# Conditioned attention on one core: the last step by halves of its queries, denominators by folds on VectorE and GpSimd

## The chip, the core and the metric

The kernel runs on one core of a Trainium2 chip. The core has engines that each work through their own queue in order: TensorE (PE in the profile; its weight loads are PEld), VectorE (DVE), ScalarE (ACT), GpSimd (POOL), and SyncE (SP), which here issues DMAs. They wait for each other through semaphores. Operands lie in SBUF, products of PE land in PSUM, which has eight banks of 512 float32 columns on 128 partitions. The metric is the device time in microseconds of one execution, as the median of several; lower is better.

## The reference

For 8 batches of 512 rows and 512 columns, 16 heads of 32 columns, `x + attention(x, cond)` is computed in float32. Cut to what matters:

```python
Q = split_heads(x @ Wq.T + bq); K = split_heads(x @ Wk.T + bk); V = split_heads(x @ Wv.T + bv)
cQ = Q + split_heads(cond @ Wq.T + bq)
cK = K + split_heads(cond @ Wk.T + bk)
attn = softmax(cQ @ cK.T / sqrt(32))          # over the keys
out = x + merge_heads(attn @ V)
```

## The kernel before

**Steps.** The work goes in 32 steps: step `t` is batch `t // 4` and a group of four heads `t % 4`, that is 128 columns of the output. In a step the scores of each head are 512 by 512. The four heads use 32 rows, or 32 columns, of PE each, so that four matmuls stand side by side. Scores are made with the keys on the partitions, so that the exponentials can go straight into the product with V, and the row maxima, found in a pass ahead, are taken off by a small bfloat16 product with ones (`onesb`). Most steps get their denominators from the exponentials of that first pass. The last two steps, 30 and 31 (`T - 2` and `T - 1`), don't: their exponentials are summed by explicit additions and a product with a matrix of ones.

**The order** is written out by hand: each engine gets its instructions in the order of the code, with `bank(i)` naming PSUM banks one by one. Code that stands later on an engine waits for all that stands ahead of it there.

**A block of keys.** `exponentials(t, kc, at)` (L748) makes the scores of 128 keys (`kc` of 0 to 3) against all 512 queries: four products with `onesb` (L753) and four of K with Q (L756), one for each head, into four banks, then four exponentials of 128x512 on ACT (L766), two heads to a chunk of 1024 columns. `times_v` (L821) multiplies such a chunk with V, four matmuls of 512 columns, adding up in one bank over the four blocks; its result has the head's 32 columns on the partitions and the queries along the free side. `times_ones` (L848) does the same with ones, which gives the denominators in the same layout.

**Sums.** `sum_of(t, to, kc, on, prs)` (L1274) adds the exponentials of block `kc` to a running sum, 128x1024 for each pair of heads, on the engine `on`. Step 30 sums in `acc`, step 31 in `acc2`. Before, one such sum of step 30 is on POOL (L1386) and all others are on DVE. For step 31 blocks 0 to 2 are added up and the fourth goes to the ones by itself (L1436).

**The end of step 30 and 31.** Step 30 is turned by DVE in 32x32 blocks (L1416, L1421), divided (L1423), its residual is added on POOL (L1424), and four DMAs store it (`store_30`, L1426). Such DMAs go by `spread`: 32 partitions, runs of 32 columns, 64 KB each. Step 31 is treated as a whole: the denominators are copied by ACT (L1442), the residual `xr` times the denominators is made by DVE (L1443), both parts of `out` times denominators are added (L1452), PE turns them back in 128x128 blocks (L920, L1454), DVE takes reciprocals (L1457) and multiplies (L1462), and two DMAs of 128 KB store them (L1468). The residual of step 31 is not loaded: it is the transposed `x` that the projections used (L195).

**What stands ahead.** The row maxima of step 31 are found during step 30 (`crossed`, L1288). `send_sums` (L1070) turns, divides and stores steps 28 and 29: DVE turns (L912), POOL multiplies and adds (L913, L914), SP issues four stores of 64 KB (L917). `late_part(i)` (L1048) names eight spare pieces of 128x512 in the store of the exponentials, and `xc` is a buffer that the last projections have left.

Of the kernel before, what the change touches and what calls it, by code (L numbers as in the profile page):

```python
# [17 lines left out]
def kernel(  # L18
# [39 lines left out]
    P = 128  # L58
# [57 lines left out]
    def banks(i, n=1):  # L116

        row = row_of[0] or [at_end[j] for j in TURNS[turn[0]]]
        j = row[i]
        if n == 1:  # L120
            return psum[:, j, :]
        k = row[i + 1]
        return psum[:, j : k + 1 : k - j, :]
# [585 lines left out]
    def split_max(t, on=nc.gpsimd):  # L709

        if t >= T:
            return
        m, sp = nmax[t], split[t % 2]
        rest = op.tile([P, NS, HG, 1], F32, tag="rest", name=f"rest_{t}")
        on.tensor_copy(sp[:, :, :, 0:1], m)
        on.tensor_tensor(rest, m, sp[:, :, :, 0:1], ALU.subtract)
        on.tensor_copy(sp[:, :, :, 1:2], rest)
        on.tensor_tensor(sp[:, :, :, 2:3], rest, sp[:, :, :, 1:2], ALU.subtract)
# [338 lines left out]
    def part_of(t, pt, of):  # L1057

        for kc in of:
            times_v(t, kc, pt, of)  # L1060
        parts[t] = stage.tile([P, NC, D], F32, tag="w", name="parts")[:, 0, :]
        nc.scalar.copy(parts[t], pt)
# [7 lines left out]
    def send_sums(t, of, den):  # L1070
        rec = op.tile([P, NB, 1], F32, tag="recs", name=f"recs_{t}")
        nc.vector.reciprocal(rec, den)
        send(t, of, rec)
# [200 lines left out]
    def sum_of(t, to, kc, on, prs=range(NP)):  # L1274
        for pr in prs:
            if kc == 1:
                on.tensor_tensor(to[pr], es[t, 0, pr], es[t, 1, pr], ALU.add)  # L1277
            else:
                on.tensor_tensor(to[pr], to[pr], es[t, kc, pr], ALU.add)  # L1279
# [5 lines left out]
    def row(i):  # L1285
        turn[0] = 8 + i

    def crossed(t, kc, qc, u=None):  # L1288


        u = u or t + 1
        open_max(u)
        bank = [banks(i) for i in range(HG)]

        def maxima(js):
            for j in js:
                row_scores(u, qc, j, banks(HG + j))

        def scores(js):
            for j in js:  # L1300
                r = slice(j * HD, j * HD + 3)
                nc.tensor.matmul(bank[j], onesb[r, :], maxT[t][r, :], start=True, stop=False)
            for j in js:
                r = slice(j * HD, (j + 1) * HD)
                nc.tensor.matmul(
                    bank[j],
                    qkT["k", t][r, kc * P : (kc + 1) * P],
                    qkT["q", t][r, :],
                    start=False,
                    stop=True,  # L1310
                )

        maxima((0, 1))
        scores((2, 3))
        scores((0, 1))
        maxima((2, 3))
        for pr in (1, 0):
            e = es[t, kc, pr] = chunk()
            for i in range(2):
                nc.scalar.activation(e[:, i, :], bank[pr * 2 + i], AF.Exp)  # L1320
        for j in range(2):
            nc.vector.tensor_reduce(
                nmax[u][:, qc, j : j + 1, 0], banks(HG + j), AX.X, ALU.max, negate=True
            )
        row_max_of(u, qc, 1, banks(HG + 2, 2))
# [54 lines left out]
    spread_sums(apart, banks(1))  # L1380
    den = denominators_of(t - 1, banks(1))
    send_sums(t - 1, whole[t - 1], den)
    row(1)
    crossed(t, 1, 2)
    acc = room_for_sums(t)
    sum_of(t, acc, 1, nc.gpsimd, [1])  # L1386
    part_of(t, banks(2), [0])
    row(2)
    crossed(t, 2, 3)
    split_max(t + 1, nc.vector)  # L1390
    pa, rest = banks(2), [1, 2, 3]
    times_v(t, 1, pa, rest)
# [2 lines left out]
    transpose_max(t + 1, bank(5), nc.vector.tensor_copy)  # L1395
    times_v(t, 2, pa, rest)
    sum_of(t, acc, 1, nc.vector, [0])
    sum_of(t, acc, 2, nc.vector)

    t = T - 1  # L1400
    exponentials(t, 0, (2, 3, 0, 1))
    times_v(t - 1, 3, pa, rest)
    nc.vector.tensor_tensor(parts[t - 1], pa, parts[t - 1], ALU.add)
    sum_of(t - 1, acc, 3, nc.vector)
    exponentials(t, 1, (7, 4, 5, 2))
    pv = bank(3)
    times_v(t, 0, pv)
    acc2 = room_for_sums(t)
    sum_of(t, acc2, 1, nc.vector)
    exponentials(t, 2, (0, 1, 7, 6))  # L1410
    times_v(t, 1, pv)
    pd = bank(5)
    times_ones(acc, pd, True, True)
    sum_of(t, acc2, 2, nc.vector)
    den = late_part(3).rearrange("p (f e) -> p f e", e=BL)
    nc.vector.transpose(den.rearrange("p f e -> p (f e)"), pd)  # L1416

    rec = op.tile([P, NB, 1], F32, tag="recs", name=f"recs_{t - 1}")
    nc.vector.reciprocal(rec, den[:, :, 0:1])
    y30 = op.tile([P, NB, BL], F32, tag="res", name=f"res_{t - 1}")  # L1420
    nc.vector.transpose(y30.rearrange("p f e -> p (f e)"), parts[t - 1])  # L1421
    x30 = xr.pop(t - 1)
    nc.vector.tensor_tensor(y30, y30, rec.broadcast_to([P, NB, BL]), ALU.mult)  # L1423
    nc.gpsimd.tensor_tensor(y30, y30, x30, ALU.add)  # L1424
# [1 line left out]
    def store_30(queue, hs):  # L1426
        b, g = divmod(t - 1, G)
        for h in hs:
            queue.dma_start(spread(out[b], g * P + h * BL), y30[h * BL : (h + 1) * BL])

    store_30(nc.sync, (0, 1))
    exponentials(t, 3, (4, 2, 0, 1))
    times_v(t, 2, pv)
    pd = bank(7)
    times_ones(acc2, pd, True, False)
    times_ones([es[t, 3, pr] for pr in range(NP)], pd, False, True)  # L1436
    times_v(t, 3, pv)

    part_x = late_part(6)
    den = late_part(5)  # L1440
    two = [slice(0, HS), slice(HS, S)]
    nc.scalar.copy(den, pd)  # L1442
    nc.vector.tensor_tensor(part_x, pd, xr[t], ALU.mult)  # L1443
    store_30(nc.scalar, (2, 3))
    oT = late_part(4)
    y = late[0][:, 1, :].rearrange("p (c s) -> p c s", c=NS)
    rec = op.tile([P, NS, HG, 1], F32, tag="rec", name="rec")
    pi, po = bank(6), [bank(4), bank(2)]
    b, g = divmod(t, G)
    untranspose(den, pi)  # L1450
    for i in range(2):
        nc.vector.tensor_tensor(oT[:, two[i]], pv[:, two[i]], part_x[:, two[i]], ALU.add)  # L1452
        for qc in (i * 2, i * 2 + 1):
            nc.tensor.transpose(  # L1454
                po[i][:, qc * P : (qc + 1) * P], oT[:, qc * P : (qc + 1) * P], ident
            )
    nc.vector.reciprocal(  # L1457
        rec, pi.rearrange("p (c h e) -> p c h e", c=NS, h=HG)[:, :, :, 0:1]
    )
    for i in range(2):  # L1460
        cs = slice(i * 2, i * 2 + 2)
        nc.vector.tensor_tensor(  # L1462
            y[:, cs].rearrange("p c (h e) -> p c h e", h=HG),
            po[i][:, two[i]].rearrange("p (c h e) -> p c h e", c=2, h=HG),
            rec[:, cs].broadcast_to([P, 2, HG, HD]),
            ALU.mult,
        )
        (nc.scalar, nc.sync)[i].dma_start(  # L1468
            out[b].rearrange("(c p) d -> p c d", p=P)[:, cs, g * P : (g + 1) * P], y[:, cs]
        )  # L1470


# [29 lines left out]
```

## Time and profile before

| | us |
|---|---|
| median of 3 runs | 649.41 (649.35 to 650.63) |
| profiled execution | 649.67 |
| its span | 647.8 |

| engine | busy us | share of the span |
|---|---|---|
| PE | 641.7 | 99% |
| DVE | 600.3 | 93% |
| ACT | 533.5 | 82% |
| POOL | 409.9 | 63% |

The span is what the profiler sees from the first to the last instruction of the program; the execution's own time is 1.87 us more. PE is busy nearly all the time, but matmuls overlap, so that a busy PE is no measure of how closely they follow each other: the starts of the groups tell that. The averages say nothing of the last 25 us, in which the change lies; there one reads the timeline, engine by engine. In the rows of the timeline the columns are the start, the time from the first start to the last end of the group, the engine and line, the operation, the names and shapes, the count, and in brackets how long the engine had been idle and what released it. One float32 matmul shows as two records.

### The profile page before, as it was taken

What the parts mean: (1) busy time and instruction counts of PE and PEld (TensorE: products, weight loads), DVE (VectorE), ACT (ScalarE), POOL (GpSimd) and SP (SyncE); (2) the same over time, 40 slices, a digit from 0 to 9 for tenths busy, and PEclk for the clock granted to TensorE, in tenths of its full rate; (3) what the DMA queues carried; (4) which work ended last, traced back from release to release, by engine and by line L of the source; (5) the groups of instructions that cost most, each with busy time, mean ns of one, the idle gap of its engine ahead of it and who ended that gap; (6) DMA issues with size and microseconds to landing.
All of it is one profiled execution on the core that took longest, in us unless ns stands there. A gap on an engine that the chain in (4) does not pass through costs nothing. (4 is left out here: it accounts for less than half of the span.)

```text
span 647.8 us, 24814 instructions
## 1 busy us (share of the span) xinstructions
PE 641.7 (99%) x9856; PEld 357.3 (55%) x9856; DVE 600.3 (93%) x845; ACT 533.5 (82%) x1364; POOL 409.9 (63%) x651
## 2 busy tenths in 40 slices
PE   9999999999999999999999999999999999999997
PEld 8445555556555555555555555555655555555541
DVE  3799999999999999999999999999999999999887
ACT  2479888889888889888888988898988888898564
POOL 3633655686765775668576776568767577675650
PEclk9999999999999999999999999999999999999999
DMA  7615588888978788877878978878898767796831
GB/s 191 107 26 85 128 164 171 172 171 191 180 158 172 161 180 175 183 165 164 185 171 174 198 150 185 165 173 169 180 195 158 156 144 163 159 189 149 192 63 34
DMA packets 248457, 102.02 MB, mean 157 GB/s; under 512 B 229962, under 2 KB 230474, under 8 KB 248340
## 3 DMA queue, kind: packets, MB, share of 16 engines
q1 hardware_dynamic: 234196, 65.54, 53.6%
q0 software_dynamic: 12384, 33.83, 20.3%
q8 instruction: 78, 1.28, 0.8%
q10 hardware_dynamic: 1760, 1.05, 0.5%
q14 instruction: 39, 0.32, 0.2%
HBM read 19.75 MB, written 8.39 MB: 43 GB/s over the span
## 5 line engine op out<-in xcount | busy, mean ns | idle before, releaser
L593 DVE TENSOR_REDUCE nmax<-psum 128x1 f32<-128x512 f32 x279 | 177.6, 675 | 9.2 <-PE psum L641 4.9
L701 ACT ACTIVATE psum<-psum,nmax 128x512 f32<-128x512 f32 x248 | 165.1, 678 | 3.6 <-DVE nmax L593 3.0
L641 PE MATMUL psum<-kT,qT 32*128 32x512 f32 x1024 | 162.0, 613 | 0.0
L701 ACT ACTIVATE store<-psum,nmax 128x512 f32<-128x512 f32 x204 | 139.5, 700 | 25.0 <-DVE nmax L593 24.8
L682 POOL DMA_DIRECT2D store<-store x258 | 128.6, 503 | 47.2 <-DMA store<-store 28.8
L799 ACT ACTIVATE store<-psum 128x512 f32<-128x512 f32 x232 | 119.8, 603 | 33.4 <-PE psum L785 33.4
L660 DVE STREAM_TRANSPOSE store<-store 128x1024 f32<-128x1024 f32 x116 | 138.9, 1217 | 0.0
L650 DVE TENSOR_REDUCE nmax<-psum 128x2 f32<-128x1024 f32 x98 | 118.9, 1213 | 0.0
L840 PE MATMUL psum<-store,v 128*32 128x256 f32 x1856 | 106.8, 381 | 0.2 <-ACT store L1320 0.2
L840 PEld LDWEIGHTS psum<-store,v 128*32 128x32 f32 x1856 | 57.3, 110 | 57.2 <-ACT wT_q L632 21.2
L913 POOL TENSOR_TENSOR res<-res,recs 128x512 f32<-128x512 f32 x30 | 31.3, 1045 | 90.8 <-DVE res L912 90.8
L785 PE MATMUL psum<-qT,kT 32*128 32x256 f32 x928 | 83.8, 374 | 0.0
L641 PEld LDWEIGHTS psum<-kT,qT 32*128 32x128 f32 x1024 | 61.6, 184 | 35.4 <-issue 17.8
L785 PEld LDWEIGHTS psum<-qT,kT 32*128 32x128 f32 x928 | 60.9, 184 | 5.6 <-issue 0.3
L701 ACT ACTIVATION_READ_ACCUMULATOR psum<-psum,nmax 128x1 f32 x248 | 55.1, 222 | 0.0
L203 POOL TENSOR_TENSOR xr<-xr,bvs 128x512 f32<-128x512 f32 x30 | 38.4, 1282 | 15.6 <-DMA x<-in_x_dram 12.8
L462 PE MATMUL psum<-wc_v,xc 128*32 128x256 f32 x768 | 47.7, 379 | 0.0
L462 PE MATMUL psum<-xc,wc_q 128*32 128x256 f32 x720 | 44.7, 379 | 0.0
L462 PE MATMUL psum<-xc,wc_k 128*32 128x256 f32 x720 | 44.5, 379 | 0.0
L701 ACT ACTIVATION_READ_ACCUMULATOR store<-psum,nmax 128x1 f32 x204 | 44.4, 217 | 0.0
L914 POOL TENSOR_TENSOR res<-res,xr 128x512 f32<-128x512 f32 x30 | 38.3, 1277 | 2.3
L462 PE MATMUL psum<-xT,wT_k 128*32 128x256 f32 x480 | 34.5, 382 | 0.0
(191 smaller groups left out, 972.5 us busy)
## 6 DMA issues: line engine op xcount, KB each, us to landing
store<-store SPq DMA_DIRECT2D x264, 128.0 KB, 2.6
store<-store POOLq DMA_DIRECT2D x258, 128.0 KB, 3.8
out_dram<-res SPq DMA_DIRECT2D x122, 64.0 KB, 3.6
xr<-in_x_dram SPq DMA_DIRECT2D x120, 64.0 KB, 4.4
x<-in_x_dram SPq DMA_DIRECT2D x112, 64.0 KB, 3.3
w_q<-in_L_cond_Wq_dram SPq DMA_DIRECT2D x4, 256.0 KB, 3.9
w_v<-in_L_cond_Wv_dram SPq DMA_DIRECT2D x16, 64.0 KB, 2.5
w_k<-in_L_cond_Wk_dram SPq DMA_DIRECT2D x16, 48.0 KB, 2.6
```

The source lines that it names most:

```text
L203: nc.gpsimd.tensor_tensor(xr[t], xr[t], bias, ALU.add)
L462: nc.tensor.matmul(pt[r], still[:, r], moving, start=(kc == kcs[0]), stop=(kc == kcs[-1]))
L593: nc.vector.tensor_reduce(nmax[t][:, qc, j : j + 1, 0], pt, AX.X, ALU.max, negate=True)
L641: nc.tensor.matmul(pt, qkT["q", t][r, qc * P : (qc + 1) * P], qkT["k", t][r, :], start=True, stop=True,)
L650: nc.vector.tensor_reduce(nmax[t][:, qc, pr * 2 : pr * 2 + 2, 0], pt, AX.X, ALU.max, negate=True)
L660: nc.vector.transpose(e, e)
L682: (nc.gpsimd if here else nc.sync).dma_start(to, of)
L701: nc.scalar.activation(to, of, AF.Exp, bias=nmax[t][:, qc, j, :], accum_out=sums[t][:, qc, j, :],)
L785: nc.tensor.matmul(banks(j)[:, i * HS : (i + 1) * HS], qkT["k", t][r, kc * P : (kc + 1) * P], qkT["q", t][r, KQ * P :], start=False, stop= ...
L799: nc.scalar.activation(e[:, j], banks(j), AF.Exp)
L840: nc.tensor.matmul(pt[j * HD : (j + 1) * HD, half * HS : (half + 1) * HS], vs[b % 2][:, kc, (g * HG + j) * HD : (g * HG + j + 1) * HD], e, ...
L914: nc.gpsimd.tensor_tensor(y, y, xr.pop(t), ALU.add)
```

## The change

Step 31 goes by halves of the queries, `q` = 0 and 1, of 256 columns, and by halves of the keys: each of the four blocks (`last_scores`) makes two key blocks of 128 against one half of the queries, which fills four banks of 512 columns as before. The products with V and with ones are of 256 columns.

For each block the two key blocks in a chunk are folded: `fold` adds the two 256-column parts of each head, 128x512 for a pair of heads. The folds of block (0, 0) go to POOL and those of (0, 1) to DVE, which then adds the two (`of_a`); those of (1, 0) go one to DVE and one to POOL (`of_b`); block (1, 1) isn't folded but goes to the ones in both parts.

The first half of the queries, `y_a`, is turned by DVE straight from PSUM, divided and given its residual by POOL, and stored by four DMAs of 32 KB on SP. Its residual, `x_a`, is loaded by four DMAs on SP behind the stores of step 29, and its bias is added on POOL behind the sum of step 30 that was on POOL before. The second half keeps the way of before, at 256 columns, with one DMA.

For step 30 the second pair's sums of blocks 2 and 3 go from DVE to POOL. Its product with ones, which stood ahead of the last scores, goes behind them and behind the ones of the first half. Its turn (L1421) comes earlier on DVE.

```diff
@@ -1380,13 +1380,24 @@
     spread_sums(apart, banks(1))
     den = denominators_of(t - 1, banks(1))
     send_sums(t - 1, whole[t - 1], den)
+    last_b, last_g = divmod(t + 1, G)
+    for h in range(HG):
+        nc.sync.dma_start(
+            late_part(7)[h * BL : (h + 1) * BL, :HS].rearrange("p (f e) -> p f e", e=BL),
+            spread(x[last_b], last_g * P + h * BL)[:, : NB // 2],
+        )
     row(1)
     crossed(t, 1, 2)
     acc = room_for_sums(t)
     sum_of(t, acc, 1, nc.gpsimd, [1])
+    x_a = late_part(7)[:, :HS].rearrange("p (f e) -> p f e", e=BL)
+    nc.gpsimd.tensor_tensor(
+        x_a, x_a, bvs[:, last_g, :].unsqueeze(1).broadcast_to([P, NB // 2, BL]), ALU.add
+    )
     part_of(t, banks(2), [0])
     row(2)
     crossed(t, 2, 3)
+    sum_of(t, acc, 2, nc.gpsimd, [1])
     split_max(t + 1, nc.vector)
     pa, rest = banks(2), [1, 2, 3]
     times_v(t, 1, pa, rest)
@@ -1395,30 +1406,117 @@
     transpose_max(t + 1, bank(5), nc.vector.tensor_copy)
     times_v(t, 2, pa, rest)
     sum_of(t, acc, 1, nc.vector, [0])
-    sum_of(t, acc, 2, nc.vector)
+    sum_of(t, acc, 2, nc.vector, [0])
+    sum_of(t, acc, 3, nc.vector, [0])
+    sum_of(t, acc, 3, nc.gpsimd, [1])
 
     t = T - 1
-    exponentials(t, 0, (2, 3, 0, 1))
+    b, g = divmod(t, G)
+    ef = {}
+
+    def last_scores(q, half, at):
+
+        bank = [bank_of(i) for i in at]
+        qs = slice(q * HS, (q + 1) * HS)
+        for j in range(HG):
+            r = slice(j * HD, j * HD + 3)
+            nc.tensor.matmul(
+                bank[j],
+                onesb[r, :],
+                maxT[t][r, qs].unsqueeze(1).broadcast_to([3, 2, HS]),
+                start=True,
+                stop=False,
+            )
+        for i in range(2):
+            kc = half * 2 + i
+            for j in range(HG):
+                r = slice(j * HD, (j + 1) * HD)
+                nc.tensor.matmul(
+                    bank[j][:, i * HS : (i + 1) * HS],
+                    qkT["k", t][r, kc * P : (kc + 1) * P],
+                    qkT["q", t][r, qs],
+                    start=False,
+                    stop=(i == 1),
+                )
+        for pr in range(NP):
+            e = ef[q, half, pr] = chunk()
+            for i in range(2):
+                nc.scalar.activation(e[:, i, :], bank[pr * 2 + i], AF.Exp)
+
+    def last_v(q, half, pt):
+        for i in range(2):
+            kc = half * 2 + i
+            for j in range(HG):
+                nc.tensor.matmul(
+                    pt[j * HD : (j + 1) * HD, :HS],
+                    vs[b % 2][:, kc, (g * HG + j) * HD : (g * HG + j + 1) * HD],
+                    ef[q, half, j // 2][:, j % 2, i * HS : (i + 1) * HS],
+                    start=(kc == 0),
+                    stop=(kc == NS - 1),
+                )
+
+    def last_ones(of, pt, start, stop):
+        for j in range(HG):
+            nc.tensor.matmul(
+                pt[j * HD : (j + 1) * HD, :HS],
+                ones[:, :HD],
+                of[j // 2][:, j % 2],
+                start=start,
+                stop=stop,
+            )
+
+    def in_two(q, half, pr):
+        return ef[q, half, pr].rearrange("p h (i s) -> p i h s", i=2)
+
+    def fold(q, half, pr, to, on):
+        e = in_two(q, half, pr)
+        on.tensor_tensor(to, e[:, 0], e[:, 1], ALU.add)
+
+    of_a = [xc[:, pr] for pr in range(NP)]
+    of_a1 = [xc[:, 2 + pr] for pr in range(NP)]
+    of_b = room_for_sums(t)[0].rearrange("p c (r s) -> p (c r) s", r=2)
+    of_b = [of_b[:, pr * 2 : pr * 2 + 2] for pr in range(NP)]
+    NH = NB // 2
+    x_a = late_part(7)[:, :HS].rearrange("p (f e) -> p f e", e=BL)
+    den_a = late_part(7)[:, HS:].rearrange("p (f e) -> p f e", e=BL)
+
+    last_scores(0, 0, (2, 3, 0, 1))
     times_v(t - 1, 3, pa, rest)
     nc.vector.tensor_tensor(parts[t - 1], pa, parts[t - 1], ALU.add)
-    sum_of(t - 1, acc, 3, nc.vector)
-    exponentials(t, 1, (7, 4, 5, 2))
-    pv = bank(3)
-    times_v(t, 0, pv)
-    acc2 = room_for_sums(t)
-    sum_of(t, acc2, 1, nc.vector)
-    exponentials(t, 2, (0, 1, 7, 6))
-    times_v(t, 1, pv)
-    pd = bank(5)
+    y30 = op.tile([P, NB, BL], F32, tag="res", name=f"res_{t - 1}")
+    nc.vector.transpose(y30.rearrange("p f e -> p (f e)"), parts[t - 1])
+    for pr in range(NP):
+        fold(0, 0, pr, of_a[pr], nc.gpsimd)
+    last_scores(0, 1, (7, 4, 5, 2))
+    pva = bank(3)
+    last_v(0, 0, pva)
+    for pr in range(NP):
+        fold(0, 1, pr, of_a1[pr], nc.vector)
+    last_scores(1, 0, (0, 1, 7, 6))
+    last_v(0, 1, pva)
+    for pr in range(NP):
+        nc.vector.tensor_tensor(of_a[pr], of_a[pr], of_a1[pr], ALU.add)
+    y_a = op.tile([P, NB, BL], F32, tag="res", name=f"res_{t}")[:, :NH]
+    nc.vector.transpose(y_a.rearrange("p f e -> p (f e)"), pva[:, :HS])
+    fold(1, 0, 0, of_b[0], nc.vector)
+    fold(1, 0, 1, of_b[1], nc.gpsimd)
+    last_scores(1, 1, (4, 5, 2, 0))
+    pda = bank(3)
+    last_ones(of_a, pda, True, True)
+    pd = bank(1)
     times_ones(acc, pd, True, True)
-    sum_of(t, acc2, 2, nc.vector)
+    nc.vector.transpose(den_a.rearrange("p f e -> p (f e)"), pda[:, :HS])
+    rec_a = op.tile([P, NB, 1], F32, tag="recs", name=f"recs_{t}")[:, :NH]
+    nc.vector.reciprocal(rec_a, den_a[:, :, 0:1])
+    nc.gpsimd.tensor_tensor(y_a, y_a, rec_a.broadcast_to([P, NH, BL]), ALU.mult)
+    nc.gpsimd.tensor_tensor(y_a, y_a, x_a, ALU.add)
+    for h in range(HG):
+        nc.sync.dma_start(spread(out[b], g * P + h * BL)[:, :NH], y_a[h * BL : (h + 1) * BL])
+
     den = late_part(3).rearrange("p (f e) -> p f e", e=BL)
     nc.vector.transpose(den.rearrange("p f e -> p (f e)"), pd)
-
-    rec = op.tile([P, NB, 1], F32, tag="recs", name=f"recs_{t - 1}")
+    rec = op.tile([P, NB, 1], F32, tag="den", name=f"recs_{t - 1}")
     nc.vector.reciprocal(rec, den[:, :, 0:1])
-    y30 = op.tile([P, NB, BL], F32, tag="res", name=f"res_{t - 1}")
-    nc.vector.transpose(y30.rearrange("p f e -> p (f e)"), parts[t - 1])
     x30 = xr.pop(t - 1)
     nc.vector.tensor_tensor(y30, y30, rec.broadcast_to([P, NB, BL]), ALU.mult)
     nc.gpsimd.tensor_tensor(y30, y30, x30, ALU.add)
@@ -1428,46 +1526,40 @@
         for h in hs:
             queue.dma_start(spread(out[b], g * P + h * BL), y30[h * BL : (h + 1) * BL])
 
+    pvb, pdb = bank(6), bank(7)
+    last_v(1, 0, pvb)
+    last_ones(of_b, pdb, True, False)
+    for i in range(2):
+        last_ones([in_two(1, 1, pr)[:, i] for pr in range(NP)], pdb, False, i == 1)
+    last_v(1, 1, pvb)
+
+    part_x = late_part(6)[:, :HS]
+    den = late_part(5)[:, :HS]
+    oT = late_part(4)[:, :HS]
+    nc.vector.tensor_tensor(part_x, pdb[:, :HS], xr[t][:, HS:], ALU.mult)
+    nc.scalar.copy(den, pdb[:, :HS])
     store_30(nc.sync, (0, 1))
-    exponentials(t, 3, (4, 2, 0, 1))
-    times_v(t, 2, pv)
-    pd = bank(7)
-    times_ones(acc2, pd, True, False)
-    times_ones([es[t, 3, pr] for pr in range(NP)], pd, False, True)
-    times_v(t, 3, pv)
-
-    part_x = late_part(6)
-    den = late_part(5)
-    two = [slice(0, HS), slice(HS, S)]
-    nc.scalar.copy(den, pd)
-    nc.vector.tensor_tensor(part_x, pd, xr[t], ALU.mult)
     store_30(nc.scalar, (2, 3))
-    oT = late_part(4)
-    y = late[0][:, 1, :].rearrange("p (c s) -> p c s", c=NS)
-    rec = op.tile([P, NS, HG, 1], F32, tag="rec", name="rec")
-    pi, po = bank(6), [bank(4), bank(2)]
-    b, g = divmod(t, G)
-    untranspose(den, pi)
+    pi, po = bank(4), bank(2)
     for i in range(2):
-        nc.vector.tensor_tensor(oT[:, two[i]], pv[:, two[i]], part_x[:, two[i]], ALU.add)
-        for qc in (i * 2, i * 2 + 1):
-            nc.tensor.transpose(
-                po[i][:, qc * P : (qc + 1) * P], oT[:, qc * P : (qc + 1) * P], ident
-            )
+        nc.tensor.transpose(pi[:, i * P : (i + 1) * P], den[:, i * P : (i + 1) * P], ident)
+    nc.vector.tensor_tensor(oT, pvb[:, :HS], part_x, ALU.add)
+    for i in range(2):
+        nc.tensor.transpose(po[:, i * P : (i + 1) * P], oT[:, i * P : (i + 1) * P], ident)
+    rec = op.tile([P, 2, HG, 1], F32, tag="rec", name="rec")
     nc.vector.reciprocal(
-        rec, pi.rearrange("p (c h e) -> p c h e", c=NS, h=HG)[:, :, :, 0:1]
+        rec, pi[:, :HS].rearrange("p (c h e) -> p c h e", c=2, h=HG)[:, :, :, 0:1]
     )
-    for i in range(2):
-        cs = slice(i * 2, i * 2 + 2)
-        nc.vector.tensor_tensor(
-            y[:, cs].rearrange("p c (h e) -> p c h e", h=HG),
-            po[i][:, two[i]].rearrange("p (c h e) -> p c h e", c=2, h=HG),
-            rec[:, cs].broadcast_to([P, 2, HG, HD]),
-            ALU.mult,
-        )
-        (nc.scalar, nc.sync)[i].dma_start(
-            out[b].rearrange("(c p) d -> p c d", p=P)[:, cs, g * P : (g + 1) * P], y[:, cs]
-        )
+    y = late[0][:, 1, :HS].rearrange("p (c s) -> p c s", c=2)
+    nc.vector.tensor_tensor(
+        y.rearrange("p c (h e) -> p c h e", h=HG),
+        po[:, :HS].rearrange("p (c h e) -> p c h e", c=2, h=HG),
+        rec.broadcast_to([P, 2, HG, HD]),
+        ALU.mult,
+    )
+    nc.sync.dma_start(
+        out[b].rearrange("(c p) d -> p c d", p=P)[:, 2:, g * P : (g + 1) * P], y
+    )
 
 
 # ---- launch: one core; inputs and outputs as the reference has them ----
```

## What was predicted from it

> **What bounds the kernel now.** I read the busy time by stretches first, then the chain that ended last, then the timeline of each engine over the last 25 us.
>
> ```profile
> 630.00:640.00 10.00, 9.92 (x92) 2.50 (x92) 10.00 (x10) 8.26 (x16) 0.00 (x0) 1.00 0.01 2
> 640.00:648.00 8.00, 3.63 (x28) 1.28 (x20) 4.03 (x10) 0.58 (x1) 1.28 (x1) 0.88 0.32 67
> ```
>
> The columns are the length, then busy us and count for PE, PEld, DVE, ACT and POOL, the granted clock, and DMA. In the last full stretch PE and DVE are both full and POOL does nothing; after 640 everything drains.
>
> ```profile
> 638.23 1.24 DVE acc L1279
> ...
> 639.51 1.48 PE psum L850 x10
> ...
> 641.42 0.86 PE psum L824 x6
> ...
> 642.89 0.76 DVE store L1452 x2
> ...
> 643.92 0.42 DVE store L1462
> ```
>
> The chain goes through DVE's last sum for the denominators, ending 639.47, then 2.77 us of PE to 642.28, then the turn, the division and the store.
>
> ```profile
> 632.28 1.08 PE L824 MATMUL psum<-store,v 128*32 128x512 f32 x8
> 633.29 0.40 PE L753 MATMUL psum<-maxT,onesb 3*128 3x512 bf16 x4
> ...
> 634.47 1.07 PE L824 MATMUL psum<-store,v 128*32 128x512 f32 x8
> 635.36 1.04 PE L850 MATMUL psum<-acc,ones 128*32 128x512 f32 x8
> 636.33 0.40 PE L753 MATMUL psum<-maxT,onesb 3*128 3x512 bf16 x4
> ...
> 637.52 1.07 PE L824 MATMUL psum<-store,v 128*32 128x512 f32 x8
> 638.40 1.73 PE L850 MATMUL psum<-acc,ones 128*32 128x512 f32 x6
> ```
>
> Starts matter here, for matmuls overlap: a burst of four 512-column products with V or the ones takes 0.88 us (637.52 to 638.40), 1.0 us ahead of a change to scores (632.28 to 633.29), and a block of scores 1.18 us (633.29 to 634.47). From 638.40 PE has three bursts, 2.6 us, and ends after 3.88: about 1.2 us are lost waiting for DVE. That loss is what the change can remove ahead of the end.
>
> **The change part by part.** *The same PE work in other pieces.* 256-column matmuls are in the trace:
>
> ```profile
> 610.64 1.04 PE L785 MATMUL psum<-qT,kT 32*128 32x256 f32 x16
> ...
> 611.61 1.07 PE L840 MATMUL psum<-store,v 128*32 128x256 f32 x16
> ```
>
> Twice as many records take the same 1.04 and 1.07 us as the 512-column rows, so halving costs nothing. The count of ones stays twelve 512-column matmuls' worth. The burst of ones for step 30 moves behind the last scores, which therefore begin at 634.47 + 1.0 = 635.47 in place of 636.33 and end at 636.65.
>
> ```profile
> 630.19 6.44 ACT L766 ACTIVATE store<-psum 128x512 f32<-128x512 f32 x12 [0.66 <-PE psum L756]
> 637.67 2.06 ACT L766 ACTIVATE store<-psum 128x512 f32<-128x512 f32 x4 [1.04 <-PE psum L756]
> ```
>
> ACT loses its 1.04 us wait: sixteen exponentials at 6.44/12 = 0.537 run through from 630.19 to 638.78. After the last scores PE has five bursts: half a burst on `of_a`, one on `acc`, one of V, half on `of_b`, one of ones and one of V, so 4.4 us. The drain is from the three-burst end of now: 2.77 - 3 x 0.88 = 0.13. Let G be the moment at which PE can take `of_a`; V ends at G + 4.5. If nothing were late, G would be near 636.65.
>
> *What `of_a` waits for.* It stands first behind the last scores, and PE works in order: the acc burst and V's third burst stand behind it. It needs two POOL folds, two DVE folds, two DVE sums of them, and the turn of `y_a` out of the same bank. POOL's queue ahead of those folds is new: the bias on `x_a`, and two sums of 128x1024.
>
> ```profile
> 622.51 1.27 POOL L914 TENSOR_TENSOR res<-res,xr 128x512 f32<-128x512 f32 x1
> ...
> 623.75 2.35 POOL L1277 TENSOR_TENSOR acc<-store 128x1024 f32<-128x1024 f32 x1
> ...
> 641.81 1.28 POOL L1424 TENSOR_TENSOR res<-res,store 128x512 f32<-128x512 f32 x1 [15.70 <-DVE res L1423]
> L913 POOL TENSOR_TENSOR res<-res,recs 128x512 f32<-128x512 f32 x30 | 31.3, 1045 | 90.8 <-DVE res L912 90.8
> ...
> L1252 POOL TENSOR_TENSOR v<-v 128x256 f32<-128x256 f32 x14 | 10.3, 733 | 1.1
> ```
>
> So POOL pays 0.73 + 2 x 2.35 + 2 x 1.28 = 7.99 us, in time that was idle (15.70). But it starts late. The `x_a` loads go on SP behind the four stores of step 29, which wait for L914:
>
> ```profile
> 626.03 0.51 SPq L917 DMA_DIRECT2D out_dram<-res  x1
> L917 SPq DMA_DIRECT2D out_dram<-res x8: 316/496/1284, 619.6 to 626.0; - x8
> L190 SPq DMA_DIRECT2D store<-in_x_dram x4: 493/648/680, 614.7 to 616.6; - x4
> DMA to landing us min/median/max: 2.5/2.8/4.4
> ```
>
> SP is free at 626.54. A 64 KB issue takes 0.32 to 0.65 us and a load lands 2.5 us or more later (the last row is L190's; stores of L917 took 1.9 to 2.2). For 32 KB I take 0.4 an issue: the last starts at 627.74 and lands at X = 630.2; the ends are 627.49 + 1.9 = 629.4 and 628.49 + 2.8 = 631.3. POOL, free at 626.10, waits 4 us, and all its sums and folds stand behind that wait. On DVE the sum of the two folds waits in turn for POOL, and behind it stand the turn of `y_a`, the second half's fold and both turns of denominators.
>
> *DVE.* It gives up five 128x1024 sums and gets small pieces.
>
> ```profile
> 628.43 1.22 DVE L1277 TENSOR_TENSOR acc<-store 128x1024 f32<-128x1024 f32 x1
> 629.68 2.36 DVE L1279 TENSOR_TENSOR acc<-acc,store 128x1024 f32<-128x1024 f32 x2
> 631.96 0.69 DVE L1403 TENSOR_TENSOR parts<-psum,parts 128x512 f32<-128x512 f32 x1
> 639.37 0.72 DVE L1416 STREAM_TRANSPOSE store<-psum 128x512 f32<-128x512 f32 x1
> 640.29 0.71 DVE L1421 STREAM_TRANSPOSE res<-parts 128x512 f32<-128x512 f32 x1
> 641.04 0.69 DVE L1423 TENSOR_TENSOR res<-res,recs 128x512 f32<-128x512 f32 x1
> ```
>
> Three sums to 632.04, L1403 and the turn of step 30 to 633.4, then folds of 0.69. A turn of 256 columns I put at 0.40 (half of 0.72 and a fixed part).
>
> *Two engines at once: the unknown.* Every DVE sum quoted that reads two SBUF tiles (L1277, L1279, L1423) ran while POOL was idle, and POOL's sum of 623.75 beside DVE reading PSUM. No row shows a two-tile DVE sum beside a POOL sum, and the new order puts them side by side. Bounds: each at its own row's duration, or one always waiting until the other's instruction is over. The nearest rows lean a little to turns: POOL's 1.28 with two tiles against 1.045 with one tile and a broadcast column (L913) says that POOL's time goes by what it reads from SBUF, and the two-tile sum is DVE's heaviest reader. Full rate for both at once is nowhere seen here. I take turns and keep the other end for the range.
>
> Side by side, G = X + 7.99 + 0.69 (second sum) + 0.40 (turn) = 639.3. In turns: DVE's second sum ends 630.86; `x_a` to 631.59; DVE's third sum 632.81; POOL's sum 635.16; DVE's fold 635.85; POOL's sum 638.20; fold 638.89; POOL's folds 640.17 and 641.45; DVE's sums 642.14 and 642.83, or 644.11 if POOL's third fold (1.28) gets in between; the turn: G = 643.2 or 644.5, I take 643.9.
>
> The Trainium skill speaks to this in "SBUF — State Buffer", section "Who interferes with whom": a VectorE instruction with two SBUF inputs contends with a GpSimd instruction that reads SBUF, and whichever comes second is blocked for the whole of the other. By that rule G is the 643.9 of the turns, without it 639.3; no run here shows it yet.
>
> *The clock.* PE would idle from 636.65 to G, 7.2 us.
>
> ```profile
> 645.80:646.00 0.20, 0.00 (x0) 0.00 (x0) 0.00 (x0) 0.00 (x0) 0.00 (x0) 1.00 1.18 343
> 646.00:646.20 0.20, 0.00 (x0) 0.00 (x0) 0.00 (x0) 0.00 (x0) 0.00 (x0) 0.63 1.14 346
> 646.20:646.40 0.20, 0.00 (x0) 0.00 (x0) 0.00 (x0) 0.00 (x0) 0.00 (x0) 0.50 0.43 118
> ```
>
> The granted clock fell to half 1.9 us after the last matmul (644.14). Return isn't shown; the bounds are nothing and all 4.4 us doubled. I take 1.9 us at half speed for the return too: +1.0 us. "TensorE: Matmul & The Clock Gate" of the Trainium skill, section "What's actually happening", asks some 3.4 us of sustained work; by that it would be +1.7, and the total 0.7 more.
>
> *The tail.* Now it runs from V's end, 642.28, to the last product's end, 644.68:
>
> ```profile
> 643.37 0.77 PE L1454 MATMUL psum<-ident,store 128*128 128x128 f32 x4 [0.51 <-DVE store L1452]
> ...
> 644.74 0.41 SPq L1468 DMA_DIRECT2D out_dram<-store  x1
> ```
>
> For half the queries it is one sum of 0.42, two transposes 0.49 (643.65 to 644.14), one product 0.42 and gaps of 0.12: 1.45 us. The early division and store of the first half (0.40, 0.25, 0.6, 0.73 and the issues) end about G + 4, under V's bursts; step 30's product and its addition end near G + 4.6, stored ahead of the last piece. The last store starts 0.06 after the product; from there to the span's end it took 3.06 us and I keep that, for it is again 128 KB behind other stores (0.5 less if less traffic matters).
>
> *Sum.* V ends 643.9 + 4.5 + 1.0 = 649.4; the span ends at 649.4 + 1.45 + 0.06 + 3.06 = 653.97, against 647.8. The profiled run took 649.67, 1.87 more than its span, and lay 0.26 above the median of 649.41, so I add 1.61: **655.6**. Ends: G 643.2 and no clock loss 653.9; G 644.5 and all doubled 659.6.
>
> **The rivals.** *Side by side* (not slower by much, or the same): G = 639.3, span 639.3 + 4.5 + 4.57 = 648.37, time 650.0. For it: the durations are rows. Against: nothing shows the pair. The idle of 2.6 us still eats the gain, since POOL began late. X from 629.4 to 631.3, 0.5 off the store and 1.0 on the clock give 648.7 to 652.1.
>
> *In time after all* (faster): side by side, and the loads land before POOL's queue needs them. Then DVE sets G: folds to 635.2, sums to 636.55, turn 636.95; V ends 641.5, span 646.1, time 647.7. The point: G passes 637.4, a gain of 1.3 us, where X is below 628.3, and G = 638.7, no gain, where X is 629.6. Against it: SP is busy to 626.54 and no landing under 1.9 us stands in the rows. For it: loads half as large.
>
> **How the numbers follow.** Turns 0.60, side by side 0.30, in time 0.10. A measurement of this kernel can tell about 0.2%, 1.3 us, from no change. Turns are slower for certain; of side by side 0.18 lies within 650.7 and 0.12 above; of the third 0.06 is faster, 0.04 within. Faster 0.06, same 0.22, slower 0.72. The range 649.3 to 658.0 leaves out the third case, a little of the second's low end and the top of the first's, under 0.2.
>
> **What would show it.** The `x_a` addition on POOL begins near 630, after a DMA; the first ones behind the last scores begin at 639 (side by side) or past 643 (turns), named as waiting for DVE; ACT's sixteen exponentials run without a gap. In turns, single DVE sums show 2 us or more in place of 0.69 beside POOL's 2.35, or POOL's show more than their rows. The granted clock is under 1.00 around 641 to 645. I am wrong if PE takes `of_a` before 638, or if DVE's folds keep 0.69 beside a running POOL sum.

## The result and the profile after

The changed kernel takes 655.85 us (median of 5, 655.4 to 657.01) against 649.50 (median of 5, 649.35 to 650.63): a ratio of 1.0095, 95% interval 1.0084 to 1.0106, that is 0.95% slower. 655.6 was forecast, in a range of 649.3 to 658.0. The profiled run took 656.48, with a span of 654.7.

The changed kernel's busy time by stretches, with the columns explained above, shows where the time went. The second stretch is 10 us long here; before, the program ended within 8.

```profile
630.00:640.00 10.00, 7.54 (x120) 3.92 (x112) 8.70 (x7) 8.58 (x17) 8.85 (x4) 1.00 0.03 5
640.00:650.00 10.00, 6.06 (x72) 2.58 (x72) 7.11 (x10) 0.03 (x1) 5.59 (x6) 0.66 0.08 13
```

PE, busy for 9.92 us of the first stretch before, stands still for 2.5 us of it and for nearly 4 of the second, and the granted clock of the second is 0.66. In the first stretch POOL is now as busy as DVE. PE's timeline says what it waited for:

```profile
636.28 0.40 PE L1423 MATMUL psum<-maxT,onesb 3*128 3x512 bf16 x4
636.50 1.03 PE L1434 MATMUL psum<-qT,kT 32*128 32x256 f32 x16
643.94 1.08 PE L1460 MATMUL psum<-xc,ones 128*32 128x256 f32 x8 [6.40 <-DVE res L1500]
644.79 1.93 PE L850 MATMUL psum<-acc,ones 128*32 128x512 f32 x8
...
649.19 1.04 PE L1450 MATMUL psum<-store,v 128*32 128x256 f32 x16
```

Behind the last scores PE stands still for 6.40 us, until DVE has turned `y_a` (L1500), the last thing ahead of the ones of `of_a`. Then a burst that took 1.04 before takes 1.93. In the queues that feed `of_a` are, on POOL and on DVE (two answers of the timeline, each row one instruction but the last of POOL's):

```profile
631.07 1.20 POOL L1394 TENSOR_TENSOR store<-store,bvs 128x256 f32<-128x256 f32 x1 [4.12 <-DMA store<-in_x_dram]
632.24 3.37 POOL L1279 TENSOR_TENSOR acc<-acc,store 128x1024 f32<-128x1024 f32 x1
635.69 2.69 POOL L1279 TENSOR_TENSOR acc<-acc,store 128x1024 f32<-128x1024 f32 x1
638.34 2.93 POOL L1473 TENSOR_TENSOR xc<-store 128x512 f32<-128x512 f32 x2
```

```profile
630.47 1.22 DVE L1279 TENSOR_TENSOR acc<-acc,store 128x1024 f32<-128x1024 f32 x1
631.79 1.57 DVE L1279 TENSOR_TENSOR acc<-acc,store 128x1024 f32<-128x1024 f32 x1
634.69 1.48 DVE L1473 TENSOR_TENSOR xc<-store 128x512 f32<-128x512 f32 x1
636.09 2.85 DVE L1473 TENSOR_TENSOR xc<-store 128x512 f32<-128x512 f32 x1
640.09 1.73 DVE L1498 TENSOR_TENSOR xc<-xc 128x512 f32<-128x512 f32 x1 [1.16 <-POOL xc L1473]
641.75 1.78 DVE L1498 TENSOR_TENSOR xc<-xc 128x512 f32<-128x512 f32 x1
```

Read the two together, by ends. DVE's second sum ends 631.69, then POOL's `x_a` 632.27; DVE's third sum 633.36, then POOL's sum 635.61; DVE's fold 636.17, then POOL's second sum 638.38; DVE's second fold 638.94. A DVE fold that takes 0.69 alone (a row of 128x512 before) shows as 2.85: it holds its place from 636.09 and gets its turn when POOL's sum is over. Each end follows the other engine's end by a little less than the instruction takes alone: 0.58 for `x_a` (0.73 alone), 1.09 for DVE's sum (1.22), 2.25 and 2.21 for POOL's sums (2.35), 0.56 for DVE's folds.

### The profile page after: what moved, and what is told of

Read it like the earlier page. It is cut to its first block, busy times and chain, and to the rows that moved or that the text cites. A ratio compares the mean times of both kernels' runs of the same rounds, so it can differ in the third digit from the quotient of the medians.

```text
span 654.7 us, 24991 instructions
## 1 busy us (share of the span) xinstructions
PE 642.9 (98%) x9932; PEld 360.2 (55%) x9932; DVE 602.4 (92%) x845; ACT 533.7 (82%) x1364; POOL 423.0 (65%) x659
## 3 DMA queue, kind: packets, MB, share of 16 engines
q8 instruction: 78, 1.28, 0.8%
## 4 chain that ended last, share of the span: by engine, by line
PE 95%; POOL 1%; DMA 1%; issue 1%; SPq 1%; DVE 1%; ACT 0%; DVEq 0%; POOLq 0%; ACTq 0%
PE psum L462 44%; PE psum L641 18%; PE psum L840 16%; PE psum L785 8%; PE psum L772 3%; PE psum L405 2%; POOL acc L1279 1%; DMA w_q<-in_L_cond_Wq_dram 1%; PE psum L824 1%; PE psum L756 1%; PE psum L313 0%; PE psum L934 0%; SPq L917 0%; PE psum L1460 0%; DMA store<-in_x_dram 0%
```

## The experiments

Each was run beside the kernel before, and the ratio is to that kernel; where a time is set against the changed kernel, which ran on another occasion, the difference by the ratios stands beside it. The theory was that two-tile sums of DVE and POOL (sums that read both operands from SBUF) take turns, whole instructions at a time, and that the clock falls in the idle behind. The rivals were the late loads of `x_a`, the strided halves, the order on PE, and halving itself.

**Turns by themselves, in the kernel before** (`e3_pool_sums`).

```diff
     sum_of(t, acc, 1, nc.gpsimd, [1])
+    beside = xc.rearrange("p a b s -> p (a b s)")[:, : 2 * S].rearrange("p (c s) -> p c s", s=S)
+    for _ in range(4):
+        nc.gpsimd.tensor_tensor(beside, wT["k"][:, :2, :], wT["k"][:, 2:, :], ALU.add)
```

> The kernel before, with four extra sums of 128x1024 on POOL behind its sum of step 30; they read two tiles of finished weights, write to a buffer that nobody reads and wait for nothing. Alone they would run from 626.1 to 635.5. Theory of turns: from 628.4 on they alternate with DVE's sums, three or four of DVE's 1.2 us sums show 2.4 us more or POOL's show 1.2 us more each, DVE's last sum ends some 6.5 us later, time 654 to 657. Rival: no row gets longer than 1.25 on DVE and 2.4 on POOL, time 649.5 within 0.5.

657.18 us, ratio 1.0116 (1.0101 to 1.0132). The size came near what was expected, but by another path. DVE's timeline, and PE's:

```profile
626.14 1.87 DVE L715 CAST split<-nmax 128x16 bf16<-128x16 f32 x1
628.04 2.37 DVE L716 TENSOR_TENSOR rest<-nmax,split 128x16 f32<-128x16 f32 x1
630.45 0.20 DVE L717 CAST split<-rest 128x16 bf16<-128x16 f32 x1
630.68 2.22 DVE L718 TENSOR_TENSOR split<-rest,split 128x16 bf16<-128x16 f32 x1
...
634.01 2.31 DVE L1277 TENSOR_TENSOR acc<-store 128x1024 f32<-128x1024 f32 x1
```

```profile
632.96 0.60 PE L737 MATMUL psum<-identb,split 128*128 128x128 bf16 x4 [6.04 <-DVE split L718]
633.50 1.94 PE L824 MATMUL psum<-store,v 128*32 128x512 f32 x8
```

Not the large sums paid first but the four pieces of 16 columns that split the row maxima, 0.18 to 0.23 us each in the kernel before; of the large sums only one then met POOL, 2.31 in place of 1.22. Of the four pieces each of three waited out one POOL sum of 2.35, and PE, which turns the split maxima, was idle for 6.04 us. Behind that idle the granted clock stayed at 0.50 until 639.2, and PE's bursts took 1.9 us in place of 1.06; so the agreement of the size with the forecast, which had neither, is luck. One of the three (L715) is a cast with a single operand: on DVE it is not only two-tile sums that are held. Nothing here is strided and no result is used, so the strided folds aren't needed for the effect. POOL's four sums kept 2.34 to 2.37 each: POOL went first, DVE paid.

**The same with writes only** (`e4_pool_writes`).

```diff
+    for _ in range(12):
+        nc.gpsimd.memset(beside, 0.0)
```

> The kernel before, with twelve extra memsets of 128x1024 on POOL at the same place as the four sums of the run before it. They write the same buffer and read nothing; at some 0.8 us each they cover 626 to 636. If it is what POOL reads that takes turns with DVE: DVE's sums stay at 1.2 us, time 649.5 within 0.5. If any POOL instruction takes turns with DVE's two-tile sums: DVE's sums show up to 0.8 us more each, time 651 to 655.

650.45 us, ratio 1.0008 (0.9999 to 1.0017). Twelve memsets of 0.95 us covered 625.8 to 637.9, and beside them stand

```profile
626.34 0.46 DVE L715 CAST split<-nmax 128x16 bf16<-128x16 f32 x1
626.84 0.19 DVE L716 TENSOR_TENSOR rest<-nmax,split 128x16 f32<-128x16 f32 x1
627.06 0.75 DVE L717 CAST split<-rest 128x16 bf16<-128x16 f32 x1
...
628.98 1.22 DVE L1277 TENSOR_TENSOR acc<-store 128x1024 f32<-128x1024 f32 x1
630.23 2.36 DVE L1279 TENSOR_TENSOR acc<-acc,store 128x1024 f32<-128x1024 f32 x2
```

The two-tile sums are untouched at their old 1.22 and 1.18, so it is what POOL reads, and not what it writes, that takes turns with them. Only the two casts were held, which I hadn't expected: 0.8 us together; the 0.5 us by which the median is higher isn't clear of no change.

**The late loads** (`e1_x_early`). The loads of `x_a` go ahead of step 29's stores on SP:

```diff
     t = T - 2
+    last_b, last_g = divmod(t + 1, G)
+    for h in range(HG):
+        nc.sync.dma_start(
...
     row(0)
...
     send_sums(t - 1, whole[t - 1], den)
-    last_b, last_g = divmod(t + 1, G)
-    for h in range(HG):
-        nc.sync.dma_start(
...
```

> The changed kernel, with the loads of x_a issued on SP ahead of step 29's stores, so that POOL finds x_a there at 626 and doesn't wait 4 us. Theory (two-tile sums of DVE and POOL take turns, whole instructions at a time): starting earlier mostly moves the collisions ahead. POOL's sums of blocks 2 and 3 now hold up DVE's three sums of step 30; DVE's addition of the parts of step 30 comes near 637 and not 633.3, and the third block of scores waits for its bank. The first ones behind the last scores begin near 641.5, time 651.5 to 653.5. Rival (POOL's late start is the cause, the long sums are a side show): POOL is through with its folds near 635, the ones begin at 637, time near 648.

654.17 us, ratio 1.0071 (1.0056 to 1.0086): 1.7 us less than the changed kernel (1.6 by the ratios) and far from the rival's 648. It is above the forecast too, for the reason that the extra sums showed: POOL, now early, met the four pieces that split the row maxima. DVE's timeline, and PE's:

```profile
627.48 0.72 DVE L717 CAST split<-rest 128x16 bf16<-128x16 f32 x1
628.24 2.30 DVE L718 TENSOR_TENSOR split<-rest,split 128x16 bf16<-128x16 f32 x1
631.31 0.42 DVE L743 COPY maxT<-psum 128x512 bf16<-128x512 bf16 x1 [0.77 <-PE psum L737]
631.65 2.33 DVE L1277 TENSOR_TENSOR acc<-store 128x1024 f32<-128x1024 f32 x1
```

```profile
630.59 0.61 PE L737 MATMUL psum<-identb,split 128*128 128x128 bf16 x4 [2.80 <-DVE split L718]
642.75 0.64 PE L1460 MATMUL psum<-xc,ones 128*32 128x256 f32 x8
```

PE was idle for 2.8 us there, and the granted clock was at 0.50 from 630.1 to 636.9. The ones of `of_a` began at 642.75 without a wait: here the loss is that idle and the half clock behind it, and no longer the wait for `of_a`. Starting POOL earlier moves the collisions, it doesn't remove them.

**The new sums and folds back on DVE** (`e2_all_dve`).

```diff
-    sum_of(t, acc, 2, nc.gpsimd, [1])
...
-    sum_of(t, acc, 2, nc.vector, [0])
-    sum_of(t, acc, 3, nc.vector, [0])
-    sum_of(t, acc, 3, nc.gpsimd, [1])
+    sum_of(t, acc, 2, nc.vector)
...
     nc.vector.tensor_tensor(parts[t - 1], pa, parts[t - 1], ALU.add)
+    sum_of(t - 1, acc, 3, nc.vector)
...
-        fold(0, 0, pr, of_a[pr], nc.gpsimd)
+        fold(0, 0, pr, of_a[pr], nc.vector)
...
-    fold(1, 0, 1, of_b[1], nc.gpsimd)
+    fold(1, 0, 1, of_b[1], nc.vector)
```

> The changed kernel, with all sums and folds that it gave to POOL back on DVE; x_a comes as late as before, and its bias is the only two-tile instruction left on POOL in that stretch. Theory of turns: DVE's sums go back to 1.2 us, its folds to 0.7, nothing is lengthened but one instruction by the bias (0.7). DVE is then the limit: the first ones begin near 641 with DVE busy all the way, 3 us sooner than in the changed kernel, time 651 to 653. Rival (the sums are long because of the strided halves they read, or because of PE and ACT working on the same store): they stay long on DVE too, the ones begin past 645, time 657 or more.

652.63 us, ratio 1.0049 (1.0032 to 1.0066), as the theory had it.

```profile
629.61 2.90 DVE L1279 TENSOR_TENSOR acc<-acc,store 128x1024 f32<-128x1024 f32 x2
...
635.93 2.45 DVE L1470 TENSOR_TENSOR xc<-store 128x512 f32<-128x512 f32 x4
638.30 1.28 DVE L1496 TENSOR_TENSOR xc<-xc 128x512 f32<-128x512 f32 x2
```

```profile
640.00 1.08 PE L1457 MATMUL psum<-xc,ones 128*32 128x256 f32 x8 [3.31 <-DVE res L1498]
```

Four folds, strided as they are, take 2.45 us, 0.61 each; only the pair that meets the bias of `x_a` shows 2.90 in place of 2.36. DVE alone does faster what the two did together, and PE's wait falls to 3.3 us.

**The order on PE** (`e5_pe_order`), with DVE and POOL as in the change:

```diff
     last_scores(1, 1, (4, 5, 2, 0))
     pda = bank(3)
-    last_ones(of_a, pda, True, True)
     pd = bank(1)
     times_ones(acc, pd, True, True)
+    pvb, pdb = bank(6), bank(7)
+    last_v(1, 0, pvb)
+    last_ones(of_a, pda, True, True)
```

> The changed kernel, with the ones of step 30 and V's third burst put ahead of the ones that wait for of_a; POOL and DVE as they are. DVE and POOL still take turns, so of_a comes near 643.9 as in the changed kernel. PE does its two bursts meanwhile (to about 640) and has 2.6 us of bursts left behind of_a in place of 4.4, 1.8 us less. If the half clock was the rest of the loss, the shorter idle (3.8 us in place of 6.4) keeps the clock mostly up and another 1 to 1.8 us go: time 652 to 653.5. If the clock falls all the same: 654 to 655. If what stands behind of_a on PE doesn't matter: 655.9.

654.88 us, ratio 1.0082 (1.0066 to 1.0097): 1.0 us less than the changed kernel (0.8 by the ratios), the middle case.

```profile
643.43 0.64 PE L1460 MATMUL psum<-xc,ones 128*32 128x256 f32 x8 [3.60 <-DVE res L1500]
644.01 0.64 PE L1460 MATMUL psum<-acc,ones 128*32 128x256 f32 x8
644.46 1.73 PE L1460 MATMUL psum<-store,ones 128*32 128x256 f32 x16
645.94 1.95 PE L1450 MATMUL psum<-store,v 128*32 128x256 f32 x16
```

```profile
649.02 0.42 DVE L1554 TENSOR_TENSOR store<-psum,rec 128x256 f32<-128x256 f32 x1 [0.33 <-PE psum L1548]
```

The idle is 3.60 us, and the last two bursts still run at half speed: the clock read 1.00 from 644.4 to 644.6 and 0.50 from 645, though PE had been at work again since 643.43. From 643.43 to the end of V at 647.89 it took 4.46 us for 2.77 of work at full speed, so the half clock cost 1.7 us, as in the changed kernel (1.76), though the idle was shorter. V ended 1.8 us sooner than there, as the bursts moved ahead had promised, once the 0.5 us by which that run is later from its start is taken off. What is missing in the time was lost behind the last product, from whose end (649.44) to the end of the span (653.0) it took 3.56 us in place of 2.91; why is not shown.

**The halves without collisions** (`e7_no_turns`). As `e2_all_dve`, with `x_a` loaded and given its bias during steps 29 and 30, and PE's free bursts first (the ones of the last block ahead of those of `of_b`).

> The changed kernel without collisions: the new sums and folds on DVE as in the run e2_all_dve, x_a loaded and given its bias during step 29 and 30, where DVE reads PSUM; and PE's bursts that wait for nothing (the ones of step 30, V's third, the ones of the last block) put ahead of those that wait. Theory (the halves cost nothing, turns and the idle behind them were the loss): DVE has all the two-tile work, of_a is ready near 639.4, PE idles about 1 us and keeps its clock; time 649.5 to 651, the same as before or a little more, for DVE's sums remain the limit. Rival (halving itself costs): 652 or more.

651.42 us, ratio 1.0028 (1.0017 to 1.0038), 0.4 above the forecast's end. The first part came as forecast, the ones of `of_a` waited for 0.92 us; the tail didn't:

```profile
639.22 0.64 PE L1457 MATMUL psum<-xc,ones 128*32 128x256 f32 x8 [0.92 <-DVE res L1498]
...
640.97 1.05 PE L1447 MATMUL psum<-store,v 128*32 128x256 f32 x16
643.83 0.44 PE L1543 MATMUL psum<-ident,store 128*128 128x128 f32 x2 [1.82 <-ACT store L1538]
```

V was through by 642.0, but DVE still had the division of step 30 to do (its product, 0.69 alone, ran 1.19 beside POOL's work on `y_a`), and the last turn waited behind that. From V's end to the end of the last product (645.15) it took 3.13 us in place of 1.56, and the clock stayed at 1.00.

**Versions that might beat both.** The chain of the kernel before went through DVE's sums. One version takes a block's two sums off DVE and lets PE add it up (`e6_before_two_plain`):

```diff
-    sum_of(t, acc2, 2, nc.vector)
...
     times_ones(acc2, pd, True, False)
+    times_ones([es[t, 2, pr] for pr in range(NP)], pd, False, False)
```

> The kernel before, with block 2 of step 31 sent to the ones as it is, like block 3, and not added up on DVE: two DVE sums less (2.4 us), one PE burst more (0.88). The chain of the kernel before went through DVE's last sum (a loss of 1.2 us on PE). V would end at 638.40 + 4 x 0.88 + 0.13 = 642.05 in place of 642.28, but DVE is free from 637.2, so step 30 is divided and stored ahead of the end, and the sum behind V starts 0.1 after V and not 0.6. Theory (DVE's sums, not PE's bursts, set the end of the kernel before): 0.7 to 1.3 us less, time 0.998 to 0.999 of before. Rival (PE sets it): no change or up to 0.9 us more.

649.29 us, ratio 0.9994 (0.9985 to 1.0003): no difference that can be told. V ended as forecast (642.52, in a run 0.5 later from its start), but DVE's part behind it started only 0.2 us sooner by the run's own start. It waited for ACT's copy of the denominators, and that for the ones, which ended at 641.66, only 0.86 us ahead of V, for PE had a burst more to do:

```profile
642.42 0.69 DVE L1443 TENSOR_TENSOR store<-psum,xT 128x512 f32<-128x512 f32 x1 [2.46 <-ACT store L1442]
```

The other goes on from the halves without collisions (`e8_whole_sums`, cut to what matters):

```diff
+    for pr in range(NP):
+        nc.vector.tensor_tensor(both[pr], ef[0, 0, pr], ef[0, 1, pr], ALU.add)
...
-    fold(1, 0, 0, of_b[0], nc.vector)
-    fold(1, 0, 1, of_b[1], nc.vector)
...
+    for i in range(2):
+        last_ones([a[:, i] for a in halves_a], pda, i == 0, i == 1)
```

> From e7_no_turns: the first half's two blocks are added whole on DVE (two sums of 128x1024, 2.4 us) and go to the ones in two parts, in place of four folds and two sums (3.7 us); the second half's third block goes to the ones without a fold (1.25 us less on DVE). PE gets two half bursts more (0.9 us). DVE's turn and division of step 30 come ahead of those of the first half. The last store goes on ACT's queue. Theory (with no turns DVE's two-tile work is what sets the end, and PE has an idle of 0.9 us to give): of_a's place is taken without a wait near 638.2, V ends near 641.8, the last product near 643.7 and its store 1.0 us ahead of that of the kernel before, ratio to before 0.998 to 0.9995. Rival (PE's two half bursts more eat it): 1.000 to 1.002.

649.67 us, ratio 1.0002 (0.9993 to 1.0011), so not the theory's number. PE waited no longer for `of_a`, and the last product ended at 643.89, 0.8 us sooner than before in a run that was 0.3 later from its start:

```profile
643.47 0.42 DVE L1552 TENSOR_TENSOR store<-psum,rec 128x256 f32<-128x256 f32 x1 [0.23 <-PE psum L1546]
```

```profile
641.39 0.85 SPq L1514 DMA_DIRECT2D out_dram<-res  x2
642.77 2.04 SPq L1523 DMA_DIRECT2D out_dram<-res  x4
```

But the "early" stores of the first half are issued on SP until 644.81, behind the last product, and by the profile SP's last wait (1.4 us) is for them. From the end of the last product to the end of the span it took 3.91 us, 3.12 before.

> e8_whole_sums, with the last stores spread over both queues: SP gets three of step 30's, two of the first half's and the last, ACT one and two. In e8_whole_sums the four stores of the first half on SP were issued until 644.81, after the last product's store (643.92), and the end waited for them. Theory (the gain at the last product was given back in that queue): the last issue is at 644.3, 0.5 to 0.8 sooner, ratio to before 0.9985 to 0.9995. Rival (the landing of the last store counts wherever it is issued, all DMA engines being full): 1.000 within 0.0005.

The same with these stores divided between SP and ACT (`e9_stores_spread`): 649.25 us, ratio 0.9994 (0.9985 to 1.0003). The last product ended at 643.52 and the last store was issued at 643.93, yet no gain can be told from no change here; from the last product to the end of the span it took 3.58 us, still 0.46 more than before. No version beat the kernel before beyond what can be measured.

## Why the prediction was right

**Halving costs nothing:** right. The last block's records are 1.03 us at 256 columns, as at 512 before, and the last scores began 0.02 off the place forecast, once the 0.79 us by which this run is later from its start (below) is taken off.

**ACT runs through:** right; twelve exponentials in 6.45, then 0.19 us of wait. (DVE gave up six sums of 128x1024, not the five that the prediction names; no term hangs on it.)

**POOL starts late:** right. `x_a` waited 4.12 us for its loads and began at 631.07, 630.28 less the 0.79, against 630.2. Two misses cancel in that: the last load was issued 0.3 us later than forecast and landed after 2.2 us, not 2.5. (The row of L917 has an issue of 1.28 us, so the 0.65 that the prediction gives as the most is not the most.) As a cause it counts less than it looks: without it 1.7 us went, not the whole, for the collisions moved to the splitting of the maxima.

**Turns or side by side:** the choice of turns was right, and the runs with extra POOL work show it, in the kernel before, where nothing else of the change is. This was the step on which the trace was silent. The Trainium skill's "SBUF — State Buffer", section "Who interferes with whom", says that a VectorE instruction with two SBUF inputs contends with a GpSimd instruction that reads SBUF and not with one that only writes it. The runs agree in both halves: DVE's 0.69 us showed as 2.85 beside a sum of POOL, and its 1.22 stayed 1.22 beside memsets.

**G:** forecast 643.9; measured 643.94, or 643.15 less the 0.79. So the sum was 0.75 us too long. POOL's third fold did come in between, as in the later of the two cases, 644.5, and by that case the sum was 1.35 too long; that 643.9 stood between the two cases made it look nearer. The mis-sized term is the price of a turn. Each was put at the full row, and a held instruction ends sooner after its turn than its row says: `x_a` 0.58 after DVE's end (row 0.73), a DVE fold 0.56 after POOL's (row 0.69). Over the eleven instructions of the chain that comes to 1.4 us.

**The clock:** the mechanism was right, the size short. From 643.94 to the end of V it took 6.29 us (650.23), 1.76 more than the 4.53 of full speed; I had put 1.0. The windows show why; the clock is the third number from the end:

```profile
640.60:640.80 0.20, 0.00 (x0) 0.00 (x0) 0.20 (x1) 0.00 (x0) 0.20 (x1) 0.83 0.00 0
640.80:641.00 0.20, 0.00 (x0) 0.00 (x0) 0.20 (x1) 0.00 (x0) 0.20 (x1) 0.50 0.00 0
...
647.20:647.40 0.20, 0.20 (x8) 0.04 (x4) 0.20 (x1) 0.00 (x0) 0.07 (x1) 0.50 0.00 0
647.40:647.60 0.20, 0.20 (x8) 0.15 (x4) 0.17 (x2) 0.00 (x0) 0.00 (x0) 0.60 0.00 0
```

It was 0.50 from about 640.7 until about 3.6 us after PE had resumed, where 1.9 had been put. The Trainium skill's "TensorE: Matmul & The Clock Gate", section "What's actually happening", asks some 3.4 us of sustained work for the return, by which the estimate would have been 1.7. This run agrees, and `e2_all_dve` with 3.0 us nearly does, but in `e1_x_early` and `e3_pool_sums` the return took 6.3 and 6.2 us from PE's restart.

**The tail:** 1.56 from V's end to the last product's (forecast 1.45), 2.91 from there to the end of the span (3.12).

Together: 653.97 forecast for the span, + 0.79 start, - 0.75 G, + 0.76 clock, + 0.11 - 0.21 for the tail, is 654.7, which was measured. The agreement within 0.3 us of the median is thus partly luck: G and the clock were each off by three quarters of a microsecond, in opposite ways. The 0.79 arises in the first 25 us, where both kernels run the same code: PE's first work on loaded weights waited 0.51 us for them in this run and 0.20 in the one before, and a second wait follows. Most of it belongs to the profiled run alone, for the run of the median has a span of 654.0.

What was not in the forecast is the worth of halving once the turns are gone. The runs answer it: nothing that can be measured (1.0002 and 0.9994). In the profiled runs, each by its own start, the last product ended 0.8 and 1.1 us sooner, and 0.8 and 0.5 of that was given back between it and the end of the span, where only stores are left.

## What to carry to other kernels

Before moving half of an addition from DVE to POOL, ask whether both operands lie in SBUF on both engines: if so, the two engines' times add, as they did here, and a DVE instruction of 0.2 us in the way can wait for a whole POOL instruction, 2.35 us here. DVE's addition of the parts of step 30, which reads one tile from PSUM, did not wait beside a POOL sum (0.68 us, 0.69 before). Where a queue of additions has a dependent at the head of PE's queue, put what is ready ahead of it; but an idle of 2.8 us or more cost again in clock in each run that had one, and one of 0.92 us did not. And a store whose data are early is only early if it is issued ahead of the last one: in `e8_whole_sums` four were issued until 644.81, the last store at 643.92.

## What was not expected of the hardware

The casts of 128x16 were held also beside memsets (0.46 and 0.75 us for 0.20), where the two-tile sums weren't. The clock went to half at different delays after PE's last matmul: 1.9 us in the kernel before, 3.2 in the changed one, and in `e5_pe_order` 1.3 us after PE had started again.

The traces together say more of this than any one of them. The stretches at half speed lasted 3.41 us (`e2_all_dve`, `e5_pe_order`), 6.82 (`e1_x_early`, the changed kernel) and 10.24 (`e3_pool_sums`), that is one, two and three times 3.41, as if the clock were set anew at fixed times 3.41 us apart, wherever PE's idle begins or ends. In the 3.41 us ahead of each fall PE was busy for 0.22 us (changed), 0.52 (`e2_all_dve`), 1.10 (`e1_x_early`), 1.25 (`e5_pe_order`) and 1.39 (`e3_pool_sums`), and 0.99 in the kernel before; in `e5_pe_order` the 3.41 us ahead of those had 1.98, and the clock stayed. It came back after 3.41 us in which PE was busy for 3.00 or more, and didn't after 2.81 and 2.93, which is too near to 3.00 to put it down to the busy time alone. No run was made to test this reading. If it holds, what an idle costs hangs also on where it falls between those times, which the program here doesn't set.
